# Block sums of k^T v in a windowed linear attention: each block's product made once, three of them added on GpSimd, two tokens taken off by one product

## The chip, the cores and the metric

The kernel runs on one core of a Trainium2 chip. The metric is the time of one execution on the device in microseconds (us), the median of several runs. Beside it stands one profiled execution, whose span and instruction records the profile and the trace show.

## The reference, cut to what matters

The network has four layers on a tensor of 4 batches x 128 channels x 64 x 64. Layers 0 and 1 (a Mamba convolution and a hypergraph convolution) come first; then the data are tokens, 4 batches of 4096 tokens with 128 features, and layers 2 and 3 are an attention and an expert layer each, with a LayerNorm ahead of both and the result added to the tokens. The change concerns the attention of layer 3, a windowed attention without a softmax:

```python
bs, w = (BLOCK_SIZE, WINDOW_SIZE)          # 256, 256
nb = S // bs                               # 16 blocks in a batch
halo = w - 1                               # 255
W = bs + 2 * halo
q = x @ Wq.T + bq
k = x @ Wk.T + bk
v = x @ Wv.T + bv
k_pad = jnp.pad(k, ((0, 0), (halo, halo), (0, 0)))
v_pad = jnp.pad(v, ((0, 0), (halo, halo), (0, 0)))
starts = jnp.arange(nb) * bs
idx = starts[:, None] + jnp.arange(W)[None, :]
k_win, v_win = k_pad[:, idx, :], v_pad[:, idx, :]
q_blk = q.reshape(B, nb, bs, -1)
scale = 1.0 / jnp.sqrt(jnp.float32(D))
attn = jnp.einsum('bnqh,bnkh->bnqk', q_blk, k_win) * scale
out = jnp.einsum('bnqk,bnkh->bnqh', attn, v_win)
...
t = t + _L3_attn_ref(_ln_t(t), L3_attn_Wq, ...)
t = t + _L3_ffn_ref(_ln_t(t), L3_ffn_gate_w, ...)
```

A block of 256 tokens attends to itself and to 255 tokens on either side. So block n sees blocks n-1, n and n+1 but for two tokens: the first token of block n-1 and the last token of block n+1. At the two ends of the sequence the missing block is zero. As there is no softmax, the order of the products is free: out = q (k_win^T v_win) x scale, with one 128x128 matrix M_n = scale x (sum of k^T v over the window's tokens) for each block.

## The kernel before, in words

`tile_kernel` (L1092) runs setup, layers 0 and 1, the first attention (`attn2`), the first expert layer (`ffn` with "L2_ffn"), the second attention (`attn3`, L827 to L909) and the second expert layer (`ffn` with "L3_ffn", which also writes the output). The tokens stay in SBUF throughout as X, 128 partitions x 4 batches x 32 blocks of 128 tokens x 128 features, f32.

The kernel is written in a tile framework. A pool hands out tiles; a tag has a number of buffers, and a tile of the same tag waits for the last reader of the buffer it gets. When a pool closes, its memory is used again by the pools that open later, and the first writer there waits for the last user before. The framework's scheduler decides the order in which instructions stand on each engine, so it isn't the order of the code: an instruction of a later batch or of the next layer can stand ahead of earlier code where its data permit. Each engine then works its queue strictly in order; an instruction that waits holds everything behind it on its engine.

`attn3` loads the three projection weights, transposes them on TensorE (`ps_w`) and loops over 4 batches. A batch has two phases.

- **Chunks.** Eight chunks of 512 tokens (L859). For every 16 blocks of 128 tokens, `ln_stats` (L695) makes the LayerNorm's statistics on VectorE (16 `bn_stats`, L700, then small operations, and a square root on ScalarE, L711). In each chunk VectorE makes four normed blocks `z` (L716, from L866), TensorE transposes them into `ps_z` (L867), ScalarE copies them to `zT` (L868), TensorE makes `ps_q` (L870, evicted by ScalarE into `qT`) and `ps_kv` in two halves (L876, four products in all), and VectorE evicts each half into `kv` with the bias added (L880). Two more VectorE operations a half make `ke` (L885): k of a block with its first token, or its last one, masked to zero.
- **Windows.** Four groups of four windows (L886). For each window TensorE adds up to six products of 128x128 in PSUM (`ps_win`, L896): two for each of the three blocks of 256 tokens, with `ke` in place of k where a token is left out. That makes 92 products in a batch and 368 in the stage. ScalarE copies the four matrices with the scale into `M` (L900), TensorE makes eight products q M (`ps_o`, L905), and VectorE adds them into X (L909).

Buffers: `kv` and `ke` have one buffer, `qT` two, `z` four, `zT` and `M` three; each of the four PSUM tags (`tr`, `ps`, `pm`, `po`) has two.

`ffn` (L911) comes twice. Its route stage handles two batches at a time: `ln_stats`, z (L969), transposes `ps_t` (L970), copies `zTf` on ScalarE and VectorE by turns (L972), the gate's product `ps_l` (L973), the eviction `lg` (L976), then over all tokens the eight largest (L980, L982), two exponentials (L986, L987), their difference (L990), transposes `ps_rt` (L997) and the pooled product `ps_p` (L1003). The experts follow, with weights loaded from HBM (L947 to L952), then the combination: in L2_ffn the products `ps_f` (L1071) and their addition into X (L1072), in L3_ffn L1078, L1082 and the output. The first expert layer thus ends with additions into X, for which the second attention waits, and the second attention ends with additions into X (L909), for which the second expert layer's statistics wait.

Of the kernel before, what the change touches and what calls it, by code (L numbers as in the profile page):

```python
# [7 lines left out]
F32 = mybir.dt.float32  # L8
F16 = mybir.dt.float16
FP8 = mybir.dt.float8e4  # L10
AF = mybir.ActivationFunctionType
ALU = mybir.AluOpType
# [4 lines left out]
P = 128  # L17
# [5 lines left out]
NB = N // P  # L23
# [5 lines left out]
def bc(ap, n):  # L29

    return ap.unsqueeze(1).to_broadcast([ap.shape[0], n, ap.shape[1]])
# [7 lines left out]
class Net:  # L39
# [787 lines left out]
    def attn3(self):  # L827


        nc, tc, a, X = self.nc, self.tc, self.a, self.X  # L830
        BS = 256
        NW = N // BS
        scale = float(C) ** -0.5
        with ExitStack() as ctx:
            wp = ctx.enter_context(tc.tile_pool(name="a3w", bufs=1))
            xp = ctx.enter_context(tc.tile_pool(name="a3x", bufs=1))
            sp = ctx.enter_context(tc.tile_pool(name="a3s", bufs=4))
            tp = ctx.enter_context(tc.tile_pool(name="a3t", bufs=3))
            ps = ctx.enter_context(tc.tile_pool(name="a3ps", bufs=2, space=PSUM))

            wT = wp.tile([P, 3, P], F32, tag="wT", name="wT3")
            pt = ps.tile([P, 3, P], F32, tag="tr", name="ps_w3")
            for k, n in enumerate("qkv"):
                w = tp.tile([P, P], F32, tag="w", name="w3")
                nc.sync.dma_start(w, a[f"L3_attn_W{n}"])
                nc.tensor.transpose(pt[:, k, :], w, self.ident)
            nc.vector.tensor_copy(wT, pt)
            bq = wp.tile([P, 1], F32, tag="bq", name="bq")
            nc.sync.dma_start(bq, a["L3_attn_bq"])
            bkv = wp.tile([P, 2, P], F32, tag="bkv", name="bkv3")  # L850
            for k, n in enumerate("kv"):
                nc.sync.dma_start(bkv[:, k, :], a[f"L3_attn_b{n}"].to_broadcast([P, P]))

            for b in range(B):
                qT = xp.tile([P, N], F32, tag="qT", name="qT3", bufs=2)
                kv = xp.tile([P, NB, 2, P], F32, tag="kv", name="kv3")

                ke = xp.tile([P, NB, P], F32, tag="ke", name="ke")
                for c in range(NCH):  # L859
                    if c % 4 == 0:  # L860
                        nm, rs = self.ln_stats(sp, b, 4 * c, 16)
                    zT = tp.tile([P, 4, P], F32, tag="zT", name="zT3")
                    pt = ps.tile([P, 4, P], F32, tag="tr", name="ps_z3")
                    for i in range(4):
                        z = sp.tile([P, P], F32, tag="z", name="z3")
                        self.normed(z, b, 4 * c + i, nm, rs, (4 * c + i) % 16)  # L866
                        nc.tensor.transpose(pt[:, i, :], z, self.ident)  # L867
                    nc.scalar.copy(zT, pt)  # L868
                    pp = ps.tile([P, CH], F32, tag="ps", name="ps_q")
                    nc.tensor.matmul(pp, wT[:, 0, :], zT.rearrange("p i c -> p (i c)"), start=True, stop=True)  # L870
                    nc.scalar.activation(qT[:, c * CH : (c + 1) * CH], pp, AF.Identity, bias=bq)
                    for h in range(2):
                        j = 4 * c + 2 * h
                        pp = ps.tile([P, 2, 2 * P], F32, tag="ps", name="ps_kv3")
                        for i in range(2):
                            nc.tensor.matmul(  # L876
                                pp[:, i, :], zT[:, 2 * h + i, :], wT[:, 1:3, :].rearrange("p k c -> p (k c)"),
                                start=True, stop=True,
                            )
                        nc.vector.tensor_tensor(  # L880
                            kv[:, j : j + 2, :, :].rearrange("p i k c -> p i (k c)"), pp,
                            bc(bkv.rearrange("p k c -> p (k c)"), 2), ALU.add,
                        )
                        for i, m in enumerate((self.notfirst, self.notlast)):
                            nc.vector.tensor_scalar(ke[:, j + i, :], kv[:, j + i, 0, :], m, None, ALU.mult)  # L885
                for g in range(NW // 4):  # L886
                    pm = ps.tile([P, 4, P], F32, tag="pm", name="ps_win")
                    for i in range(4):
                        n = 4 * g + i
                        terms = [(kv[:, 2 * n, 0, :], 2 * n), (kv[:, 2 * n + 1, 0, :], 2 * n + 1)]  # L890
                        if n > 0:
                            terms += [(ke[:, 2 * n - 2, :], 2 * n - 2), (kv[:, 2 * n - 1, 0, :], 2 * n - 1)]
                        if n < NW - 1:
                            terms += [(kv[:, 2 * n + 2, 0, :], 2 * n + 2), (ke[:, 2 * n + 3, :], 2 * n + 3)]
                        for t, (kk, j) in enumerate(terms):
                            nc.tensor.matmul(  # L896
                                pm[:, i, :], kk, kv[:, j, 1, :], start=t == 0, stop=t == len(terms) - 1
                            )
                    M = tp.tile([P, 4, P], F32, tag="M", name="M")
                    nc.scalar.activation(M, pm, AF.Copy, scale=scale)  # L900
                    for h in range(2):
                        po = ps.tile([P, 4, P], F32, tag="po", name="ps_o3")
                        j = 8 * g + 4 * h
                        for i in range(4):
                            nc.tensor.matmul(  # L905
                                po[:, i, :], qT[:, (j + i) * P : (j + i + 1) * P], M[:, 2 * h + i // 2, :],
                                start=True, stop=True,
                            )
                        nc.vector.tensor_tensor(X[:, b, j : j + 4, :], X[:, b, j : j + 4, :], po, ALU.add)  # L909
# [241 lines left out]
```

## Time and profile before

| | |
|---|---|
| runs | 4511.88, 4515.98, 4558.93 us; median 4515.98 us |
| the profiled execution's own time | 4506.08 us |
| its span in the trace | 4504.3 us |
| TensorE (PE) busy | 3713.7 us, 82% of the span |
| VectorE (DVE) busy | 3124.2 us, 69% |
| GpSimd (POOL) busy | 2415.8 us, 54% |
| ScalarE (ACT) busy | 1981.6 us, 44% |
| second attention | 3963.76 to 4197.06 us |

How to read it: the page gives the busy time of each engine, summed over the whole span, so 82% is a mean over stages that have different limits. The trace gives the same by stretches of time, and the chain of waits follows the work that ended last back from the end, at each step to what released it. In a group of instructions the columns are the line and engine, the operation with output and inputs, the number of records, the busy time in us with the mean of one in ns, and the idle time of the engine just before. A TensorE product of f32 operands leaves two records.

### The profile page before, as it was taken

Reading aid. Unit: us, or ns where it says so; the run is one execution under the profiler, and the core shown is the slowest. Engines: PE = TensorE matmul, PEld = TensorE weight load, DVE = VectorE, ACT = ScalarE, POOL = GpSimd, SP = SyncE. Lnnn points to the kernel's source line nnn. Section 1 sums busy time; section 2 is a strip of 40 time slices with the busy share of each in tenths; the row PEclk is TensorE's granted clock in tenths of the full one; section 3 lists DMA queues with packets and bytes.
Section 4 is the critical chain, followed back from the end, with each engine's and each line's share of the span. In section 5 each row is a group of like instructions: output and inputs, shape, how many; then the busy total and the mean of one; then the engine's idle time right before and its main releaser. Section 6 shows DMA issues by size and latency. Waiting matters only on the chain. (4 is left out here: it accounts for less than half of the span.)

```text
span 4504.3 us, 50176 instructions
## 1 busy us (share of the span) xinstructions
PE 3713.7 (82%) x17975; PEld 2095.2 (47%) x17975; DVE 3124.2 (69%) x5140; ACT 1981.6 (44%) x3104; POOL 2415.8 (54%) x1182
## 2 busy tenths in 40 slices
PE   6887768888887888887878888899977995899778
PEld 2333233345433434543434454456535763578435
DVE  5888889997668999666999866453118985287621
ACT  4655554456445445644544564213225643022221
POOL 5999889887777888677888877300021000000000
PEclk8988878999998899998889999999988997789878
DMA  3455544454464445455455535312250000800044
GB/s 102 155 150 150 143 114 139 124 148 132 126 189 114 125 130 154 122 151 164 113 132 138 153 107 169 119 61 77 76 200 31 1 2 6 297 2 1 2 172 166
DMA packets 261741, 524.36 MB, mean 116 GB/s; under 512 B 21706, under 2 KB 24306, under 8 KB 261490
## 3 DMA queue, kind: packets, MB, share of 16 engines
q1 hardware_dynamic: 250194, 501.78, 37.9%
q10 hardware_dynamic: 11296, 19.37, 1.3%
q8 instruction: 142, 2.33, 0.2%
q14 instruction: 109, 0.89, 0.1%
HBM read 443.47 MB, written 77.59 MB: 116 GB/s over the span
## 5 line engine op out<-in xcount | busy, mean ns | idle before, releaser
L284 POOL TENSOR_TENSOR db<-dx,bt 128x1024 f32<-128x1024 f32 x512 | 1203.0, 2353 | 331.7 <-DVE hs L302 214.6
L302 DVE TENSOR_TENSOR_SCAN hs<-hs,carry,db 128x512 f32<-128x512 f32 x812 | 1035.2, 1282 | 177.5 <-ACT hs L296 95.2
L296 ACT ACTIVATE hs<-dl,A 128x512 f32<-128x512 f32 x1024 | 706.6, 692 | 740.6 <-DVE ho L312 687.1
L497 PE MATMUL ps_g<-xn 128*128 128x512 f32 x1152 | 602.5, 654 | 99.8 <-DVE inc L500 74.3
L319 POOL TENSOR_TENSOR ho_s<-ho_s,ho 128x1024 f32<-128x1024 f32 x288 | 677.1, 2351 | 13.8 <-DVE ho L312 13.1
L312 DVE TENSOR_TENSOR ho<-hs,bt 128x1024 f32<-128x1024 f32 x464 | 563.2, 1214 | 1.6
L520 PE MATMUL ps_ed<-xs,inc 128*128 128x258 f16 x4096 | 513.6, 286 | 18.3 <-ACT inc L513 8.6
L520 PEld LDWEIGHTS <-inc 128*128 128x128 fp8e4 x4096 | 417.8, 102 | 134.6 <-issue 60.6
L500 DVE SCALAR_TENSOR_TENSOR inc<-ps_g,hcl,hb 128x512 fp8e4<-128x512 f32 x576 | 420.3, 736 | 36.7 <-PE ps_g L497 20.9
L497 PEld LDWEIGHTS ps_g<-xn 128*128 128x128 f32 x1152 | 216.0, 204 | 416.6 <-DVE inc L500 182.9
L340 PE MATMUL ps_y<-ho,cst 128*128 128x512 f32 x512 | 274.0, 678 | 108.9 <-POOL ho L308 91.5
L620 PE MATMUL ps_v<-inc_v,es 128*128 128x512 fp8e4 x1536 | 343.1, 383 | 19.2 <-DMA bt<-bcd 17.3
L620 PEld LDWEIGHTS <-es 128*128 128x128 f16 x2048 | 202.7, 99 | 288.9 <-issue 64.1
L513 ACT CAST inc<-ps_t 128x512 fp8e4<-128x512 f32 x448 | 232.1, 600 | 94.5 <-PE ps_t L509 94.3
L222 PE MATMUL ps_c<-xt,wc 128*128 128x512 f32 x512 | 234.9, 613 | 12.6 <-DVE inc L500 6.8
L340 PEld LDWEIGHTS ps_y<-ho,cst 128*128 128x128 f32 x512 | 105.1, 214 | 269.0 <-POOL ho L308 122.6
L526 ACT COPY ed<-ps_ed 128x129 f32<-128x129 f32 x128 | 34.0, 266 | 383.7 <-PE ps_ed L520 383.7
L527 DVE TENSOR_TENSOR ed<-ps_ed,ed 128x129 f32<-128x129 f32 x128 | 36.6, 286 | 211.8 <-ACT ed L526 208.8
L302 DVE TENSOR_TENSOR_SCAN hs<-hs,db 128x512 f32<-128x512 f32 x116 | 141.2, 1223 | 53.6 <-POOL db L284 42.6
L536 POOL TENSOR_TENSOR ed<-ed,rdeg 128x512 f32<-128x512 f32 x32 | 33.3, 1039 | 250.7 <-DVE rdeg L532 250.7
L222 PEld LDWEIGHTS ps_c<-xt,wc 128*128 128x128 f32 x512 | 99.8, 198 | 140.2 <-issue 119.2
L509 PE MATMUL ps_t<-ident,strip 128*128 128x128 fp8e4 x1344 | 115.1, 227 | 51.4 <-ACT inc L513 16.9
(262 smaller groups left out, 5785.5 us busy)
## 6 DMA issues: line engine op xcount, KB each, us to landing
bt<-bcd SPq DMA_DIRECT2D x512, 512.0 KB
inc<-inc SPq DMA_DIRECT2D x192, 256.0 KB
inc_v<-inc SPq DMA_DIRECT2D x96, 512.0 KB
w<-in_L_ffn_weight SPq DMA_DIRECT2D x32, 1024.0 KB
w2f<-in_L_ffn_weight SPq DMA_DIRECT2D x32, 1024.0 KB
strip<-inc SPq DMA_DIRECT2D x84, 256.0 KB
x<-x ACTq DMA_DIRECT2D x32, 256.0 KB
xn<-x SPq DMA_DIRECT2D x32, 256.0 KB
```

Of the source, the lines that this page charges most:

```text
L222: nc.tensor.matmul(s["ps"][h], wc[:, h, j, :], xt[:, j : j + T], start=j == 0, stop=j == 3)
L284: nc.gpsimd.tensor_tensor(db, s["dx"], bc(s["bt", n][:, 0, :], 2), ALU.mult)
L296: act(nc.scalar.activation(hs[:, k, :], s["dl"][:, k, :], AF.Exp, scale=A[:, k, n : n + 1]))
L302: nc.vector.tensor_tensor_scan(to[:, h, :], hs[:, h, :], db[:, h, :], init, ALU.mult, ALU.add)
L312: nc.vector.tensor_tensor(ho, hs, ct, ALU.mult)
L319: nc.gpsimd.tensor_tensor(s["sum", n // G], s["sum", n // G], ho, ALU.add)
L340: nc.tensor.matmul(s["y"][h], self.ident, t[:, h, :], start=False, stop=n == DS - 1 and k == len(terms) - 1,)
L497: nc.tensor.matmul(pq, xn[v // 4][:, v % 4 * P : (v % 4 + 1) * P], xn[c], start=True, stop=True)
L500: nc.vector.scalar_tensor_tensor(inc[:, v, :], pq, hc[:, v : v + 1], hb, ALU.subtract, ALU.is_gt, saturate=False)
L513: later(1, lambda: act(nc.scalar.copy(inc[:, v, :], pt, saturate=False)))
L520: nc.tensor.matmul(pe[:, : 2 * P + 2], inc[:, v, i * P : (i + 1) * P], xs[:, v, :], start=v == 0, stop=v == NB - 1,)
L620: nc.tensor.matmul(pv, es[:, e, k, :], inc[:, e, :], start=e == 0 and k == 0, stop=e == NB - 1 and k == 1,)
```

## The change

The attention's result is the same; the window's matrix is made in another way.

- Each block of 256 tokens gets its product k^T v once: two products of 128x128 (`ps_bl`, L900 of the changed kernel), two blocks in each chunk, right after the chunk's `kv`. ScalarE evicts them with the scale into `bl` (L901), which has a zero block at either end.
- After a batch's chunks, four GpSimd operations (L904 to L907) fill `two`: for each window, k and v of the first token of block n-1 in partitions 0 to 31 and of the last token of block n+1 in partitions 96 to 127. The k part is multiplied with a mask that is -scale on that token and zero elsewhere. Each operation covers 32 partitions x 15 windows x 128 elements. The rest of `two` is set to zero once, by GpSimd (L862).
- For each window one product of `two` (`ps_win`, L911) gives minus the two left-out tokens' part. GpSimd adds the three blocks of `bl` in two additions of 128x512 for a group of four windows (L913, L914), and VectorE adds `ps_win` to it (L915), which gives `M`. `ps_o` and the addition into X stay (L920, L924).
- `ke` and its operations are gone. `two` and `bl` have one buffer each.

Lines of `ffn` stand 15 lower in the changed kernel (L980 is L995).

```diff
@@ -851,11 +853,20 @@
             for k, n in enumerate("kv"):
                 nc.sync.dma_start(bkv[:, k, :], a[f"L3_attn_b{n}"].to_broadcast([P, P]))
 
+
+            masks = wp.tile([P, 2], F32, tag="masks", name="masks")
+            for i, m in enumerate((self.notfirst, self.notlast)):
+                nc.vector.tensor_scalar(masks[:, i : i + 1], m, 1.0, scale, ALU.subtract, ALU.mult)
+
+            two = xp.tile([P, NW, 2, P], F32, tag="two", name="two")
+            nc.gpsimd.memset(two, 0.0)
+
+            bl = xp.tile([P, NW + 2, P], F32, tag="bl", name="bl")
+            nc.gpsimd.memset(bl[:, 0, :], 0.0)
+            nc.gpsimd.memset(bl[:, NW + 1, :], 0.0)
             for b in range(B):
                 qT = xp.tile([P, N], F32, tag="qT", name="qT3", bufs=2)
                 kv = xp.tile([P, NB, 2, P], F32, tag="kv", name="kv3")
-
-                ke = xp.tile([P, NB, P], F32, tag="ke", name="ke")
                 for c in range(NCH):
                     if c % 4 == 0:
                         nm, rs = self.ln_stats(sp, b, 4 * c, 16)
@@ -881,23 +892,27 @@
                             kv[:, j : j + 2, :, :].rearrange("p i k c -> p i (k c)"), pp,
                             bc(bkv.rearrange("p k c -> p (k c)"), 2), ALU.add,
                         )
-                        for i, m in enumerate((self.notfirst, self.notlast)):
-                            nc.vector.tensor_scalar(ke[:, j + i, :], kv[:, j + i, 0, :], m, None, ALU.mult)
+
+                    pm = ps.tile([P, 4, P], F32, tag="pm", name="ps_bl")
+                    for i in range(2):
+                        for h in range(2):
+                            k, v = (kv[:, 4 * c + 2 * i + h, m, :] for m in range(2))
+                            nc.tensor.matmul(pm[:, i, :], k, v, start=h == 0, stop=h == 1)
+                    nc.scalar.activation(bl[:, 2 * c + 1 : 2 * c + 3, :], pm[:, :2, :], AF.Copy, scale=scale)
+                kw = kv.rearrange("p (w i) k c -> p w i k c", i=2)
+                lo, hi = slice(0, 32), slice(96, P)
+                nc.gpsimd.tensor_scalar(two[lo, 1:, 0, :], kw[lo, : NW - 1, 0, 0, :], masks[lo, 0:1], None, ALU.mult)
+                nc.gpsimd.tensor_copy(two[lo, 1:, 1, :], kw[lo, : NW - 1, 0, 1, :])
+                nc.gpsimd.tensor_scalar(two[hi, : NW - 1, 0, :], kw[hi, 1:, 1, 0, :], masks[hi, 1:2], None, ALU.mult)
+                nc.gpsimd.tensor_copy(two[hi, : NW - 1, 1, :], kw[hi, 1:, 1, 1, :])
                 for g in range(NW // 4):
                     pm = ps.tile([P, 4, P], F32, tag="pm", name="ps_win")
                     for i in range(4):
-                        n = 4 * g + i
-                        terms = [(kv[:, 2 * n, 0, :], 2 * n), (kv[:, 2 * n + 1, 0, :], 2 * n + 1)]
-                        if n > 0:
-                            terms += [(ke[:, 2 * n - 2, :], 2 * n - 2), (kv[:, 2 * n - 1, 0, :], 2 * n - 1)]
-                        if n < NW - 1:
-                            terms += [(kv[:, 2 * n + 2, 0, :], 2 * n + 2), (ke[:, 2 * n + 3, :], 2 * n + 3)]
-                        for t, (kk, j) in enumerate(terms):
-                            nc.tensor.matmul(
-                                pm[:, i, :], kk, kv[:, j, 1, :], start=t == 0, stop=t == len(terms) - 1
-                            )
+                        nc.tensor.matmul(pm[:, i, :], two[:, 4 * g + i, 0, :], two[:, 4 * g + i, 1, :], start=True, stop=True)
                     M = tp.tile([P, 4, P], F32, tag="M", name="M")
-                    nc.scalar.activation(M, pm, AF.Copy, scale=scale)
+                    nc.gpsimd.tensor_tensor(M, bl[:, 4 * g : 4 * g + 4, :], bl[:, 4 * g + 1 : 4 * g + 5, :], ALU.add)
+                    nc.gpsimd.tensor_tensor(M, M, bl[:, 4 * g + 2 : 4 * g + 6, :], ALU.add)
+                    nc.vector.tensor_tensor(M, pm, M, ALU.add)
                     for h in range(2):
                         po = ps.tile([P, 4, P], F32, tag="po", name="ps_o3")
                         j = 8 * g + 4 * h
```

## The prediction

> **What bounds the kernel now.** I read the page first: span 4504.3 us, TensorE busy 82%, VectorE 69%, GpSimd 54%. These are averages over stages with different limits, so I next took busy time by stretch over the second attention alone. By the chain of waits it runs from 3963.76 us (last product of the first expert layer, `ps_f`) to 4197.06 us (last addition into X): 233.3 us. The rows cut it at the first `ps_z` of each batch, with the start-up in front and the first expert stage behind.
>
> ```profile
> core 0: us, PE busy (x) PEld busy (x) DVE busy (x) ACT busy (x) POOL busy (x), PEclk, DMA share, GB/s
> 3963.76:3972.04 8.28, 0.93 (x5) 0.51 (x4) 7.81 (x40) 1.59 (x2) 0.00 (x0) 0.50 0.09 16
> 3972.04:4027.58 55.54, 55.23 (x349) 45.63 (x349) 53.77 (x236) 13.52 (x25) 0.00 (x0) 0.96 0.00 1
> 4027.58:4083.08 55.50, 55.16 (x361) 46.09 (x361) 43.58 (x169) 13.78 (x26) 0.00 (x0) 1.00 0.01 1
> 4083.08:4138.57 55.49, 55.26 (x360) 46.14 (x360) 36.61 (x122) 12.65 (x22) 0.00 (x0) 1.00 0.00 1
> 4138.57:4197.06 58.49, 56.88 (x372) 47.62 (x372) 39.67 (x132) 12.61 (x21) 0.00 (x0) 1.00 0.00 1
> 4197.06:4227.92 30.86, 24.75 (x97) 10.19 (x97) 24.11 (x91) 10.35 (x18) 0.00 (x0) 1.00 0.02 4
> ```
>
> TensorE is busy from edge to edge in every batch (55.2 of 55.5 us) and GpSimd does nothing. The chain confirms it; this is one chunk and the window phase of the second batch:
>
> ```profile
> 4053.67 0.67 PE ps_win L896 x6
> 4054.34 1.08 PE ps_q L870 x2
> 4055.42 1.91 PE ps_kv L876 x8
> 4057.32 0.33 PE ps_z L867 x3
> ...
> 4063.20 6.25 PE ps_win L896 x56
> 4069.46 1.85 PE ps_o L905 x16
> 4071.30 5.36 PE ps_win L896 x48
> 4076.66 1.84 PE ps_o L905 x16
> ```
>
> A product of 128x128 f32 is two records, and dense records follow each other every 5.36/48 = 0.112 us, so one product costs 0.223 us. Note that some `ps_win` (x6 to x8) stand inside the chunks: the windows start while the projections still run. The groups of the stage (all of 233.3 us) give the counts:
>
> ```profile
> L896 PE MATMUL ps_win<-kv 128*128 128x128 f32 x496 | 79.7, 275 | 0.0
> L700 DVE BATCH_NORM_STATS2 lnst<-X 128x6 f32<-128x128 f32 x249 | 53.1, 277 | 0.3
> L896 PE MATMUL ps_win<-kv,ke 128*128 128x128 f32 x240 | 46.4, 275 | 0.0
> ```
>
> Here 496+240 = 736 records are 368 products. The 249 statistics are 128 for this stage and 121 that belong to the expert layer behind it: VectorE takes them early, in its idle time.
>
> **What the Trainium skill says.** "GPSIMD Engine Reference", Elementwise and Engine selection: two-input operations cost some 2.6 cycles an element at 1.2 GHz, one-input ones run at about line rate. The trace agrees on the first (128x1024 takes 2353 ns, 2.8 cycles; 128x512 took 1039 ns on L536) and shows no large one-input operation. "SBUF — State Buffer", Who interferes with whom: GpSimd and VectorE lock each other out of a shared port pair if VectorE runs a 2-port mode or reads two SBUF tensors. VectorE here reads PSUM and SBUF, or one SBUF tensor; z of 128 elements takes 340 ns. "VectorE: DVE Perf Modes", the errata section, has (N+151)/0.96: 290 ns at 128, and by the same form 224 ns with half the cycles, so z does not look like a 2-port operation. "TensorE: Matmul & The Clock Gate", Part 1: idle of about 3.4 us halves the clock. Agreed: 8.28 us of idle in the first row stand at clock 0.50, and the first `ps_q` after it took 1.73 us in the chain against 0.86 later.
>
> **The change, part by part.** I used the order in which each engine's instructions stand in the two built programs; nothing differs ahead of the end of the first expert layer (about 3936 us).
>
> (1) TensorE. Out: 368 products x 0.223 = 82.1 us. In: 128 block products and 64 two-token products, 192 x 0.223 = 42.9. Saved 39.2 us, all on the path. A batch then needs 8 chunks x (1.04 q + 1.91 kv + 0.44 z) = 27.1, plus 32 block products 7.1, 16 window products 3.6, 32 `ps_o` 7.4 = 45.2 us, where it was 55.5.
>
> (2) Start-up. In the new order the first batch's statistics and z stand between the X additions of the layer before, where VectorE idles 0.33 or 1.15 us before each; two statistics (0.2 us each) fit. Now `ps_q` starts at 3974.10, 10.3 us after the stage's start. After: wait for the last X addition 0.8, `ps_w` 0.9, four z 0.45, zT copy and latencies 0.75 = 2.9 us. Gain 7.4 us.
>
> (3) The new wait. Four GpSimd operations of 32 partitions x 1920 elements fill `two` once the batch's last kv is evicted, and every `ps_win` of the batch stands behind them on TensorE. Not in the trace. Bounds for one: line rate 1920/1.2 GHz = 1.6 us below (estimate from the skill), the two-input price of L536, 1039/512 x 1920 = 3.9 us, above. I take 2.0, as the work has one input, plus some start cost: 8.0 for four. Counting from the last chunk's kv product: first eviction at 1.9, so GpSimd ends at 1.9+8.0+0.2 = 10.1. TensorE has kv 1.91, bl 0.9, z 0.44, then q 0.95 and kv 1.91 of the next batch, to 6.1, and 12 more z (1.3). Idle: 2.7 us. Behind it on TensorE are q, all `ps_o` and the next batch's bl. VectorE too waits for GpSimd, at the next batch's first kv eviction (`kv` has one buffer), then does two evictions and M: 0.8 us more of waits. So 3.5 us at each of three boundaries, 10.5.
>
> (4) Last batch. Nothing fills: idle to 10.1 is 6.5; then M, `ps_o` and X additions alternate, VectorE's M addition (0.7) now standing between `ps_win` and `ps_o` and behind the earlier X additions: 2.8 more. 9.3 us.
>
> (5) Hidden. The sums for M, 32 GpSimd additions of 1.04 us, are ready early for three groups of four; the fourth stands behind the `two` operations and ends at 10.1+2.1, or once its M buffer is free, before VectorE wants it. The 128 `ke` operations go (30.1 us of VectorE) and are worth nothing, as VectorE isn't the bound; if it were, they'd pay for the 16 M additions (11 us) anyway. ScalarE's 32 evictions of 128x256 replace 16 of 128x512; it is busy 13 of 55 us. The memset of `two` has the first batch's time.
>
> Stage after: 2.5 (start-up without z) + 4x45.2 + 10.5 + 9.3 = 203 us, so 30 us less.
>
> (6) Given back behind it. The new tiles take more SBUF. In the built program the expert layer's first statistic waits for the last M addition, since its tile lies in that memory: the 121 early statistics all move behind the attention. Up to the first maximum (L980) VectorE then has 78 statistics x 0.195 = 15.2, 64 z x 0.27 = 17.3, 8 zTf 5.5, four chains of small operations 2.5: 40.5 us, where the last row shows 30.9. With about 1.5 us of waits for the square roots: 11 us lost. The remaining 50 lie beside the 9 us of exponentials and the 14 us of `ps_rt`/`ps_p`. The expert weights' first loads also move behind the attention; they are needed 137 us later. Seven DMA issues on ScalarE (0.5 to 0.65 us each) come before its first square root, and end as the statistics do.
>
> Sum: 30 - 11 = 19 us. The profiled 4506.08 us (span 4504.3 and 1.8 around it) becomes 4487; it lies 10 us under the median of the three runs, 4515.98, so the time to expect is 4497.
>
> **Rivals.** (B) GpSimd is slow, and the change costs time. Each us more for one `two` operation costs 4x4 = 16 us, so it decides from 2.0+19/16 = 3.2 us on. At the two-input price of 3.9: +30, 11 us slower than before, 4527. For it: the 2.3 ns an element that GpSimd shows, and no one-input row that says otherwise. Against: only one input to read.
> (C) No stall to speak of: `two` at line rate, z covers the wait, and the late statistics sit in TensorE's gaps (24.8 of 30.9 us busy). Then idle falls 6 us, the loss at the back from 11 to 5: 4485. For it: VectorE has been idle 6.8 us of that row. Against: those gaps are waits for VectorE's own results.
> (D) Ports and clock: z are held while GpSimd runs, after all, and the last batch's and the expert stage's idle halve the clock. 14 z late by 2.6 us at three boundaries is 8, clock 3 x 2 us is 6: 4511.
>
> **How the numbers follow.** The forecast 0.50 (4488 to 4508 by itself), B 0.22, C 0.13, D 0.15. The range goes to the two-input price and a little beyond (4532), and at the lower end to C with 9 us for the scatter of runs (4476). One per cent, 45 us, is about what a measurement of this kernel can tell from no change: faster by more asks for all of (1) and (2) with nothing given back, 0.05; slower by more asks for 6 us for each `two` operation, 0.06; within it 0.89.
>
> **What would show it.** Right: `ps_q` some 3 us after the last `ps_f`; 384 records of `ps_bl` and `ps_win`; TensorE idle 2 to 4 us before `ps_win` with GpSimd named as releaser, 6 to 7 in the last batch; 128 statistics in the stage and the rest behind it; the expert layer's first maximum some 41 us after the last X addition. Wrong: `two` operations far from 2.0 us; z longer than 340 ns beside GpSimd; a wait of ScalarE for GpSimd at the `bl` evictions that holds q or zT.

## The result, and the profile after

Over 22 runs of each kernel the median went from 4517.97 to 4581.34 us, and the ratio of the undisturbed runs is 1.0084 (95% interval 1.0054 to 1.0113): some 38 us slower, between 24 and 51. Forecast were 19 us less, so the change ended on the other side. The medians also hold executions in which TensorE's clock in the last stage was about halved (0.53 in the changed kernel's first profile, 0.97 in that of before) and this stage took 136 to 142 us instead of some 80, as it did in the profiles of stats_early, z_act and the three kernels below whose names begin with actc_stats; the ratio leaves most such executions out, and the profile below is a second one of the changed kernel, taken without that (4522.92 us, span 4521.1).

Busy time by stretch, cut where TensorE starts again after its wait at the end of a batch: the start-up to the first `ps_q`; the first batch's chunks; then twice the windows of one batch with the chunks of the next; the third batch's windows with the whole of the fourth; and the route stage to the first maximum. Columns are the stretch, its length, then busy time and records of PE, PEld, DVE, ACT and POOL, TensorE's granted clock, DMA share and GB/s.

```profile
core 0: us, PE busy (x) PEld busy (x) DVE busy (x) ACT busy (x) POOL busy (x), PEclk, DMA share, GB/s
3966.16:3969.66 3.50, 2.23 (x9) 1.84 (x10) 3.13 (x10) 0.58 (x1) 3.43 (x3) 0.50 0.22 40
3969.66:4021.71 52.05, 40.92 (x192) 29.04 (x191) 47.92 (x149) 15.14 (x30) 21.44 (x10) 0.89 0.00 0
4021.71:4079.34 57.63, 49.77 (x281) 39.11 (x282) 47.92 (x108) 14.46 (x28) 24.02 (x12) 0.91 0.00 1
4079.34:4136.92 57.58, 49.83 (x274) 38.65 (x273) 38.72 (x61) 13.02 (x25) 23.98 (x12) 0.89 0.00 1
4136.92:4207.78 70.86, 56.54 (x341) 46.63 (x339) 30.53 (x54) 10.15 (x20) 26.41 (x14) 0.87 0.00 1
4207.78:4259.89 52.11, 33.63 (x97) 12.79 (x97) 39.99 (x183) 11.33 (x20) 0.00 (x0) 0.74 0.25 83
```

TensorE issues far less (274 to 281 records from one boundary to the next, 360 before), yet that takes 57.6 us where it took 55.5, because TensorE is idle for 7.8 us of it and runs at 0.9 of its clock. From the last addition of the layer before to the last addition into X it is 241.6 us (before 232.6 by the same cut), and from there to the first maximum 52.1 (30.9). The first profile of the changed kernel has 241.7 and 52.1. These two stretches give 9 + 21 = 30 us, within the interval of the ratio; the later stages differ from before by no more than the two profiles of the changed kernel differ there.

The chain of waits at the second boundary:

```profile
4061.78 1.92 PE ps_kv L887 x8
...
4067.07 10.46 DVE z L716 x6
...
4077.66 1.68 PE ps_z L878 x6
```

and at the end of the last batch:

```profile
4178.85 1.00 POOL two L904
...
4183.92 1.77 POOL two L905
...
4185.77 5.12 POOL two L906
...
4190.93 1.79 POOL two L907
...
4192.77 2.93 PE ps_win L911 x12
```

In the last batch TensorE has almost nothing left to do: of the 13.9 us from GpSimd's first operation to the windows it is idle for 12.5. At the inner boundaries the chain names z of VectorE instead. What GpSimd does in that time is in its timeline:

```profile
4063.47 5.11 POOL L904 TENSOR_SCALAR two<-kv,masks 32x1920 f32<-32x1920 f32 x1 [0.83 <-DVE kv L891]
4068.55 1.81 POOL L905 COPY two<-kv 32x1920 f32<-32x1920 f32 x1
4070.43 5.17 POOL L906 TENSOR_SCALAR two<-kv,masks 32x1920 f32<-32x1920 f32 x1
4075.65 1.78 POOL L907 COPY two<-kv 32x1920 f32<-32x1920 f32 x1
```

and VectorE's:

```profile
4064.33 14.97 DVE L716 TENSOR_SCALAR z<-X,lnnm,lnrs 128x128 f32<-128x128 f32 x14
```

The two multiplications take 5.1 us each, more than the upper bound of 3.9, and the two copies 1.8; the four take 13.85 us, where the prediction had 8.0. Beside them fourteen z, which need about 0.27 us each when dense, take 15 us. By source line the stage's z read

```profile
L716 DVE TENSOR_SCALAR z<-X,lnnm,lnrs x124: 324/340/5069, 3967.6 to 4171.1; 128x128 f32<-128x128 f32 x124
```

(shortest, median and longest in ns; before, the longest was 347). The longest z is as long as a GpSimd multiplication. The groups of the stage, against those of the prediction:

```profile
L900 PE MATMUL ps_bl<-kv 128*128 128x128 f32 x256 | 41.5, 286 | 0.6 <-DVE kv L891 0.5
L700 DVE BATCH_NORM_STATS2 lnst<-X 128x6 f32<-128x128 f32 x95 | 22.2, 285 | 0.0
L911 PE MATMUL ps_win<-two 128*128 128x128 f32 x128 | 21.4, 335 | 12.2 <-POOL two L907 12.2
```

256 + 128 = 384 records replace 736, as worked out. A `ps_win` takes 335 ns in the mean instead of 275, because the first group of windows behind a wait runs slowly. At the second boundary the clock was 1.00 in the 4.3 us ahead of the wait; then 16 records of `ps_win` took 3.41 us in the chain, at clock 0.50, and the next 16, some 8 us later, 1.79 us at 1.00:

```profile
4079.34:4082.75 3.41, 3.41 (x18) 3.41 (x17) 1.85 (x3) 0.14 (x1) 0.00 (x0) 0.50 0.02 5
4087.73:4089.52 1.79, 1.79 (x18) 1.71 (x17) 1.38 (x2) 0.00 (x0) 0.93 (x1) 1.00 0.00 0
```

The statistics in the stage are 95 instead of 249.

### The profile page after: what moved, and what is told of

It is laid out like the page before. It is cut to its first block, busy times and chain, and to the rows that moved or that the text cites. A ratio compares the mean times of both kernels' runs of the same rounds, so it can differ in the third digit from the quotient of the medians.

```text
span 4602.8 us, 49529 instructions
## 1 busy us (share of the span) xinstructions
PE 3759.7 (82%) x17623; PEld 2098.7 (46%) x17623; DVE 3142.6 (68%) x5030; ACT 1984.6 (43%) x3120; POOL 2516.6 (55%) x1233
## 5 line engine op out<-in xcount | busy, mean ns | idle before, releaser
L222 PE MATMUL ps_c<-xt,wc 128*128 128x512 f32 x512 | 237.4, 618 | 13.9 <-DVE inc L500 6.8
L862 POOL MEMSET two<- 128x4096 f32 x1 | 3.5, 3512 | 333.9 <-ACT lnrs L711 333.9
```

What stands on the lines that cost most here:

```text
L222: nc.tensor.matmul(s["ps"][h], wc[:, h, j, :], xt[:, j : j + T], start=j == 0, stop=j == 3)
```

## The experiments

Theory: three things, in order of size. The wait for `two` is long because a GpSimd multiplication costs 5.1 us; the expert layer's late statistics cost 21 us; and GpSimd's work holds z, which adds a little. Rivals: the hold of z is the main cost, or TensorE's clock and the sums on GpSimd are.

Each run is read by the two stretches in its own profile: in the two profiles of the changed kernel they repeat to 0.1 us, while the start of the attention lies anywhere from 3947 to 3988 us in the profiles here. Times in us; ratio is of the undisturbed runs to those of before, with its 95% interval, where there were enough.

| kernel | four operations on two | attention | to the first maximum | both | ratio |
|---|---|---|---|---|---|
| before | none | 232.6 | 30.9 | 263.4 | 1 |
| the change | 13.85, GpSimd | 241.6 | 52.1 | 293.7 | 1.0084 (1.0054 to 1.0113) |
| stats_early | 13.85, GpSimd | 240.8 | 37.2 | 278.0 | 1.0105 (1.0055 to 1.0155) |
| z_act | 13.85, GpSimd | 235.0 | 50.8 | 285.8 | one run |
| two_tt | 10.3, GpSimd | 230.7 | 51.8 | 282.5 | one run |
| two_copy | 7.1, GpSimd | 216.6 | 50.8 | 267.4 | one run |
| two_act4 | 7.3, ScalarE | 227.1 | 51.8 | 278.8 | 1.0065 (1.0040 to 1.0090) |
| actc | in chunks, ScalarE | 198.3 | 51.0 | 249.3 | 0.9976 (0.9943 to 1.0009) |
| actc_stats | in chunks, ScalarE | 197.2 | 34.2 | 231.4 | 0.9830 (0.9736 to 0.9924) |
| actc_stats_sumdve | in chunks, ScalarE | 195.3 | 35.0 | 230.2 | none |
| actc_stats_sumdve_zact | in chunks, ScalarE | 209.1 | 34.3 | 243.3 | 0.9932 (0.9869 to 0.9995) |
| kinds (of before) | see below | 237.1 | 50.8 | 287.8 | 1.0069 (1.0023 to 1.0114) |

**after_again**: the changed kernel, no edit.

> The changed kernel once more, for a second profile. If the stretch of the attention and of the route stage behind it are what makes it slower, both read as in the first profile (about 242 us from the last addition of the layer before to the last addition into X, and about 52 us from there to the first maximum), and nothing else differs by more than 5 us from the kernel before. If the cost lies in TensorE's clock in the last stage (62 pairs of ps_f at 4.0 us in the first profile, 2.1 us before), the attention and route stretches still differ but the sum of all stages doesn't match.

The first reading held for the two stretches: 241.6 and 52.1 us. The last stage takes 80.1 us (before 80.5), so nothing is lost there. That nothing else would differ by more than 5 us did not hold: the expert stage, from its first `ps_eo` to the first `ps_f`, takes 74.7 us here, 89.8 before and 93.6 in the first profile of the changed kernel. That is why this profile's span is only 17 us above that of before; since two profiles of one kernel differ there by 19 us, it isn't put down to the change.

**kinds**: GpSimd's price by kind of operation, and what it holds, on the kernel before.

```diff
+dead = xp.tile([P, 15, P], F32, tag="dead", name="dead")
...
+lo = slice(0, 32)
+nc.gpsimd.tensor_copy(dead[lo, 0, 0:1], kv[lo, NB - 1, 1, 0:1])
+for r in range(4):
+    src = X[lo, 3, 0:15, :]
+    if b == 0:
+        nc.gpsimd.tensor_scalar(dead[lo], src, self.notfirst[lo], None, ALU.mult)
+    elif b == 1:
+        nc.gpsimd.tensor_copy(dead[lo], src)
+    elif b == 2:
+        nc.gpsimd.tensor_tensor(dead[lo], src, src, ALU.add)
+    else:
+        nc.gpsimd.tensor_scalar(dead[lo], kv[lo, 0:15, 0, :], 2.0, None, ALU.mult)
```

> The kernel before, with four GpSimd operations of 32 partitions x 1920 elements after each batch's last kv, into a dead tile that nobody reads: batch 1 multiplies with a per-partition operand, batch 2 copies, batch 3 adds two inputs, batch 4 multiplies with a constant. Theory 1 (an operation has its price by kind, and VectorE's z waits for the whole of a GpSimd operation): 5.1, 1.8 and about 4 us, the constant like the operand; single z of about the length of the GpSimd operation beside them; yet the attention stays within 3 us of 233, since TensorE has window products to work on meanwhile, so being held is not what costs. Theory 2 (being held costs): the attention grows by 5 to 10 us. Theory 1 for the statistics: the dead tile takes memory, so the expert layer's statistics stand behind the attention here too, and the time grows by 15 to 21 us though the attention's own products are those of before.

The records of the dead tile (durations in ns, shortest, median, longest):

```profile
L892 POOL TENSOR_SCALAR dead<-X,cst x4: 5107/5108/5112, 4022.0 to 4037.6; 32x1920 f32<-32x1920 f32 x4
L894 POOL COPY dead<-X x4: 1773/1775/1776, 4085.6 to 4091.1; 32x1920 f32<-32x1920 f32 x4
L896 POOL TENSOR_TENSOR dead<-X x4: 3375/3376/3377, 4141.1 to 4151.5; 32x1920 f32<-32x1920 f32 x4
L898 POOL TENSOR_SCALAR dead<-kv x4: 5033/5034/5035, 4196.6 to 4211.9; 32x1920 f32<-32x1920 f32 x4
```

An operation with a scalar costs 2.7 ns an element whether the scalar is an operand or a constant, a copy 0.9, and the addition of a tile to itself 1.8. So the price doesn't go by the number of inputs: the dearest kind and the cheapest have one each. No z fell beside them here, but other work of VectorE's did:

```profile
4022.26 4.99 DVE L886 TENSOR_SCALAR ke<-kv,cst 128x128 f32<-128x128 f32 x2
...
4037.91 3.33 DVE L707 TENSOR_TENSOR lnrs<-lnst 128x16 f32<-128x16 f32 x1
```

Two `ke` took 0.46 us elsewhere in this trace and a `lnrs` 0.17. So operations with scalars from SBUF to SBUF, and one with two SBUF inputs, lasted until GpSimd's instruction ended, whatever their own size. Not all did: another `lnrs` and two `lnd` beside GpSimd kept their 0.17 to 0.18 us. The additions into X, which read PSUM, keep their 0.69 us in the same stretch. The attention grew by 4.5 us, between the two expectations, so this run doesn't say what a hold costs. It does show the other loss alone: with the attention's own products unchanged, the dead tile moved the statistics behind it and the stretch to the first maximum went from 30.9 to 50.8 us.

**two_tt** and **two_copy**: the wait for two shortened in two steps.

```diff
-nc.gpsimd.tensor_scalar(two[lo, 1:, 0, :], kw[lo, : NW - 1, 0, 0, :], masks[lo, 0:1], None, ALU.mult)
+nc.gpsimd.tensor_tensor(two[lo, 1:, 0, :], kw[lo, : NW - 1, 0, 0, :], mk[lo, 0, :, :], ALU.mult)
```

for two_tt, where `mk` is the mask broadcast over windows and row, and for two_copy, which leaves the mask out,

```diff
-nc.gpsimd.tensor_scalar(two[lo, 1:, 0, :], kw[lo, : NW - 1, 0, 0, :], masks[lo, 0:1], None, ALU.mult)
+nc.gpsimd.tensor_copy(two[lo, 1:, 0, :], kw[lo, : NW - 1, 0, 0, :])
```

with the same in `two[hi]`.

> The changed kernel with the mask multiplied by a two-input operation of GpSimd (the mask broadcast over the row) instead of the operation with a per-partition operand; the result is the same. If the price goes by the kind of operation, as in the run of the four kinds (3.4 us for two inputs, 5.1 with an operand), the four take 10.3 us a batch and the attention falls by 4 x 3.5 = 14 us, to 225 to 231 us. If the broadcast input costs as much as the operand did, nothing changes.

> The changed kernel with the two multiplications by a mask replaced by plain copies on GpSimd; this leaves the mask out, so 32 tokens are taken off at each end of a window instead of one. The four operations then take 4 x 1.8 = 7.2 us a batch instead of 13.8, near the 8.0 us that the prediction took. Theory 1 (the price of the multiplication is what the prediction missed): 6.6 us less in each of four batches, so the attention falls by 20 to 28 us, to 214 to 222 us. Rival (the hold of z, TensorE's clock and the sums would have kept it long at the predicted price too): it stays above 228 us.

The multiplications took 3.38 us as two-input operations, and 1.78 us as copies. The attention of two_copy, with the columns as above:

```profile
3957.94:4174.56 216.62, 197.93 (x1091) 155.46 (x1091) 149.61 (x378) 53.42 (x102) 72.22 (x51) 0.93 0.01 1
```

From 13.85 to 10.3 to 7.1 us a batch the attention goes from 241.6 to 230.7 to 216.6: 25.0 us for 6.7 us less in four batches, 3.7 us for each us (3.1 in the first step, 4.4 in the second). Theory 1 holds for the size: the price, with the wait and the hold that come of it, is worth 25 us of the attention.

**two_act4**: the same four operations on ScalarE.

```diff
-nc.gpsimd.tensor_scalar(two[lo, 1:, 0, :], ..., masks[lo, 0:1], None, ALU.mult)
-nc.gpsimd.tensor_copy(two[lo, 1:, 1, :], ...)
+nc.scalar.activation(two[lo, 1:, 0, :], ..., AF.Identity, scale=masks[lo, 0:1])
+nc.scalar.copy(two[lo, 1:, 1, :], ...)
```

> The four operations on two go to ScalarE, same shapes; GpSimd keeps the sums. Theory 1 (the wait is GpSimd's own speed, 13.8 us a batch): an operation takes 1.5 to 2.0 us, the wait for two falls to 6 to 8 us a batch, z is no longer held by them, and the time falls by 20 to 30 us. Rival 1 (the cost is elsewhere: late statistics and TensorE's clock after any idle): the attention falls by less than 10 us. Rival 2 (ScalarE's queue: zT, qT and bl stand behind the four operations): the time falls by 5 to 15 us only, and TensorE waits for zT.

They take 1.9 and 1.77 us there, 7.3 together, and the attention falls by 14.5: less than theory 1 said, and 10.5 us longer than two_copy with the same total on GpSimd. Rival 2 is right about the order, but not about the wait. At the second boundary ScalarE's next copy of `zT` starts only when the fourth operation ends (4077.9 us), so TensorE has no products of the next batch to fill the time with; the wait that it shows is for `two`, not for zT: 5.5 to 5.7 us in each batch, 22.3 in all, where in two_copy the waits at the ends of the four batches, for z or `two`, add up to 13.8. That is 8.5 of the 10.5 us.

**z_act**: z on ScalarE, so that GpSimd can't hold it.

```diff
-self.normed(z, b, 4 * c + i, nm, rs, (4 * c + i) % 16)
+nc.scalar.activation(z, X[:, b, 4 * c + i, :], AF.Identity, bias=nr[:, q : q + 1], scale=rs[:, q : q + 1])
```

> The changed kernel with z made on ScalarE (one operation with scale and bias a block, as many as before), so that VectorE's z can't be held by GpSimd; the GpSimd operations stay at 5.1 and 1.8 us. In the changed kernel TensorE's window products wait for two until it is done, and for the held z 1.9 us more. Theory 1 (the speed of the four operations is the cost, the hold adds little): the attention falls by 3 to 10 us from 241.6, no more. Rival (the hold is the main cost): it falls by over 15 us, towards the 227.1 us of the run with the four operations on ScalarE.

```profile
3970.67:4205.68 235.01, 193.54 (x1091) 155.49 (x1091) 101.24 (x255) 96.66 (x226) 98.86 (x51) 0.90 0.01 1
```

6.6 us less, within theory 1's 3 to 10. What TensorE waits for shows why; these are the longest sums of waits in the attention, of the changed kernel and of z_act (us in total, times, longest):

```profile
PE ps_z L878 <- DVE z L716: 26.6, 12, 8.0
PE ps_win L916 <- POOL two L912: 34.0, 4, 12.2
```

Of the 26.6 us, 25.4 lie at the three inner boundaries. With no z to hold, TensorE waits there for `two` itself, 34.0 less the 12.2 of the last batch = 21.8 us. So although the chain named z, `two` would have been late almost as long: the hold is real and secondary. The 6.6 us are a net figure, since z on ScalarE has a cost of its own (the last run below).

**stats_early**: the expert layer's statistics in a pool of their own, opened ahead of the attention.

```diff
+net.s3 = ctx.enter_context(tc.tile_pool(name="s3", bufs=4))
 net.attn3()
...
-st[r] = self.ln_stats(sp, 2 * p + r, 4 * c, 16)
+st[r] = self.ln_stats(sp if out is None else self.s3, 2 * p + r, 4 * c, 16)
```

> The changed kernel with the expert layer's LayerNorm statistics in memory of their own, so that they needn't wait for the last M addition. Theory 1 (late statistics cost what the profile shows, 52 us instead of 31 to the first maximum): some 100 statistics move into the attention, the stretch falls to 33 to 36 us and the time by 15 to 20 us. Rival (VectorE is blocked by GpSimd inside the attention, so early statistics only lengthen it): the stretch falls as well, but the attention grows by as much, and the time moves by less than 5 us.

The stretch fell from 52.1 to 37.2 us, a little above the 33 to 36 expected, and the attention didn't grow (240.8), so the early statistics are free and late ones cost 15 of the 21 us. What is left shows in the chain:

```profile
4228.17 4.88 DMA gw<-in_L_ffn_gate_w
```

The gate's weights are loaded only at the end of the attention, in both kernels; now the first expert weights, moved to the same moment, share the DMA engines with them (34% busy in this stretch, 2% before). That the sharing makes the load slow is likely, but no run keeps the two apart. The ratio doesn't show the gain: at 1.0105 (1.0055 to 1.0155) its interval overlaps that of the change. Stretches outside the change move by more than this gain (the start of the attention above), so the claim rests on the profile alone.

**actc** and **actc_stats**: k and v of the left-out tokens made on ScalarE in each chunk, right after its `kv`; the sums stay on GpSimd.

```diff
-nc.vector.tensor_scalar(masks[:, i : i + 1], m, 1.0, scale, ALU.subtract, ALU.mult)
+nc.vector.tensor_scalar(masks[:, i : i + 1], m, 1.0, -(scale ** 0.5), ALU.subtract, ALU.mult)
...
+n = min(2 * c + 3, NW)
+nc.scalar.activation(two[lo, 2 * c + 1 : n, :, :], kw[lo, 2 * c : n - 1, 0, :, :], AF.Identity, scale=masks[lo, 0:1])
+n = max(2 * c - 1, 0)
+nc.scalar.activation(two[hi, n : 2 * c + 1, :, :], kw[hi, n + 1 : 2 * c + 2, 1, :, :], AF.Identity, scale=masks[hi, 1:2])
...
-nc.vector.tensor_tensor(M, pm, M, ALU.add)
+nc.vector.tensor_tensor(M, M, pm, ALU.subtract)
```

> As actc_stats without the separate memory for the statistics, so they stand behind the attention again. Theory 1 (the two losses are independent): the attention takes 192 to 200 us, as in actc_stats or a little less, the stretch to the first maximum 50 to 53 us instead of 34, and together they are 245 to 252 us: with the wait for two gone the change is faster than before (263.5 us) even with the late statistics. Rival (the statistics inside the attention are what lengthens it): the attention falls to under 187 us.

> The two left-out tokens' k and v are made on ScalarE chunk by chunk (two operations of 32 partitions x 512 each chunk, k and v scaled alike with the square root of the scale, and the product subtracted), so that the last part is ready about 1 us after the last kv; statistics in memory of their own; the sums stay on GpSimd. Theory 1 (waiting for two is what made the attention long): TensorE's idle time in the attention falls from 42 to under 20 us, its clock rises from 0.88 to over 0.95, the attention takes 200 to 212 us, the stretch to the first maximum 33 to 38 us, and both together are 20 to 30 us less than before the change (263.5 us). Rival (the sums on GpSimd, 1.27 us each, hold z and come late themselves): the attention stays over 220 us, and TensorE waits for M.

The two stretches of actc_stats:

```profile
3976.22:4173.46 197.24, 184.93 (x1091) 148.66 (x1091) 160.31 (x501) 95.57 (x170) 44.20 (x35) 0.98 0.01 2
4173.46:4207.62 34.16, 26.47 (x97) 10.92 (x97) 23.66 (x85) 10.17 (x17) 0.00 (x0) 0.90 0.38 127
```

TensorE's idle time is 197.24 - 184.93 = 12.3 us where it was 42.3, and its clock 0.98. The attention is somewhat below the low end of theory 1; both stretches are 32 us shorter than before the change, where 20 to 30 were expected. The measured ratio is 0.983 (0.9736 to 0.9924), faster than before by 0.8 to 2.6%; 32 us are 0.7%, just outside it. The ratio rests on two executions of this kernel, and what else was shorter in them isn't known, so the stretches are the safer size. Without the separate memory (actc) the attention is the same and the stretch behind it 51.0, so the two losses are independent; that kernel's ratio, 0.9976, can't be told from before.

**actc_stats_sumdve** and **actc_stats_sumdve_zact**: the sums on VectorE, then z on ScalarE as well.

```diff
-nc.gpsimd.tensor_tensor(M, bl[:, 4 * g : 4 * g + 4, :], bl[:, 4 * g + 1 : 4 * g + 5, :], ALU.add)
-nc.gpsimd.tensor_tensor(M, M, bl[:, 4 * g + 2 : 4 * g + 6, :], ALU.add)
+nc.vector.tensor_tensor(M, bl[:, 4 * g : 4 * g + 4, :], bl[:, 4 * g + 1 : 4 * g + 5, :], ALU.add)
+nc.vector.tensor_tensor(M, M, bl[:, 4 * g + 2 : 4 * g + 6, :], ALU.add)
```

> As actc_stats, with the sums on VectorE instead of GpSimd (32 additions of 128x512, 0.7 us each). If GpSimd's sums cost anything (held z, late M), the attention is 3 to 10 us shorter than in actc_stats. If VectorE becomes the bound (22 us more work on it), it is longer, and fewer statistics stand early.

> As actc_stats_sumdve, with z on ScalarE too. If VectorE is the bound there, this takes 36 us of work off it and the attention gets 3 to 10 us shorter. If ScalarE's queue becomes the bound (z, zT, qT, two and bl in order, some 27 us a batch more), it gets longer.

The sums on VectorE gave 2 us, under the 3 that were expected if GpSimd's sums cost anything: they are all but hidden. With z on ScalarE too the attention is 14 us longer: ScalarE's busy time there rises from 96 to 144 us, and TensorE now waits 8.5 us for its `qT` and 7.2 for its `zT`. What was taken off VectorE didn't show, as VectorE wasn't the bound.

## Why the prediction was wrong

**Where it failed.** Step (3): "I take 2.0, as the work has one input, plus some start cost". The two copies cost that (1.8 us), the two multiplications 5.1: a mean of 3.46 us, past the 3.2 from which rival (B) was said to decide. The bounds were also too low, since the upper one came from a two-input operation and was taken for the dearest kind. By the slope of two_copy, 3.7 us of attention for each us a batch, (13.85 - 8.0) x 3.7 = 22 us of the 39 by which the stage lies over the 203 forecast (242.3 us from the last `ps_f`, as the prediction cut it).

**The other 17 us of the attention.** The 203 us were 181 us of products, four times the "45.2 us" of step (1), and some 22 us of waits. The changed kernel has 199.3 us busy and 42.3 idle. In two_copy, with 7.1 us for the four operations instead of 8.0, the idle time is 216.6 - 197.9 = 18.7 us; 0.9 us more in each of four batches gives some 22 (an estimate from these rows). At the right price the waits of (2) to (4) would thus have come out. TensorE's busy time would not: it stays at 197.9 us. So the second failed step is the 45.2 us a batch in (1), the price of dense products for a TensorE that now stops at the end of each batch. In actc_stats, where it doesn't wait for `two`, as many records are busy 184.9 us, at clock 0.98. The halved clock behind each wait is a part of the difference that is shown (1.6 us for the first 16 `ps_win` of the second boundary, and the `ps_z` ahead of them stand at 0.50 too); how the rest divides between the clock and short gaps inside the chunks, the runs don't separate.

The prediction knew of a halved clock, but carried it only in rival (D), with 6 us. What it took as agreement in its first row isn't: of the "8.28 us of idle" 0.93 are busy, and the clock had been at 0.50 before, with TensorE busy all the time:

```profile
3940.00:3963.76 23.76, 23.76 (x133) 23.05 (x132) 11.66 (x17) 0.00 (x0) 0.00 (x0) 0.50 0.00 1
```

It had also dismissed the hold, because a z of 340 ns "does not look like a 2-port operation". A duration taken with nothing beside it can't show that, and the section that it cites gives (N+151)/0.96 for an f32 addition of two tensors, not for z's operation. What the Trainium skill says in "SBUF — State Buffer", Who interferes with whom, fits what the trace now shows: the one blocks the other for the whole of an instruction, and `tensor_scalar` is named there among the operations that can take the shared pair (z up to 5069 ns against 347). By z_act it cost little beside the wait for `two`.

**Step (6), the statistics.** This is the third failed step. The mechanism was right, and is shown alone by stats_early and by kinds; the size was off, 21.2 us for 11. VectorE's work was 40.0 us against 40.5 forecast. The wrong term is "about 1.5 us of waits": it is 12.1 us (52.1 - 40.0). The largest in VectorE's timeline are these:

```profile
4212.89 0.23 DVE L70 COPY gwT<-ps_tr 128x64 f32<-128x64 f32 x1 [3.34 <-PE ps_tr L69]
...
4250.89 0.69 DVE L987 COPY zTf<-ps_t 128x512 f32<-128x512 f32 x1 [2.92 <-PE ps_t L985]
```

The first is the late load of the gate's weights, the others copies that stand in VectorE's order ahead of what it could do. The row of before already had 30.86 - 24.11 = 6.7 us of such waits, which should have been carried along.

**What held.** (1): 384 records instead of 736. (2): the first `ps_q` starts 3.5 us after the last addition into X, 4.2 after the last `ps_f`; 2.9 were forecast and 10.3 before, so 6 us gained for 7.4. (4) had the right shape, and its wait for two is 12.5 us idle instead of 6.5. (5): the sums and M are all but hidden, as actc_stats_sumdve shows, though an addition took 1.27 us instead of 1.04. At the second boundary TensorE idles 7.8 us (15.0 us with 7.2 busy), at the others 9.9 and 7.7, where 2.7 were forecast.

**The rivals.** (B) happened, with the hold and the halved clock of (D) on top. (B) gave 4527 us for 3.9 us an operation, 11 over before; at a mean of 3.46 it was 30, since (B) carried over the sum's other shortfalls. The "Elementwise" and "Engine selection" sections of the "GPSIMD Engine Reference", from which the 2.0 came, give 2.6 cycles an element for two inputs and about line rate for one; here a copy agrees with the second (0.93 ns an element), and an operation with a scalar, one input too, costs 2.66 ns, 3.2 cycles at the page's 1.2 GHz.

## What to carry to other kernels

An engine's price goes by the kind of operation; where the trace has no row of that kind, put the dearest known row's price well inside the range, and keep what waits for it short by making it in pieces as its input arrives: here the same work in chunks on ScalarE, with the statistics early again, turned a loss of 30 us over the two stretches into a gain of 32. When a new tile grows a pool, look at what in the next layer was early because that memory was free. If a chain names one engine, ask what else was late at that moment: z ended last, yet with z made elsewhere TensorE waited for `two` instead, 21.8 of the 25.4 us. And price the products behind a new wait at the pace that they have there, not at the dense one: the busy time fell by 24 us (223.4 to 199.3), where 39 were forecast.

## What the runs showed of the hardware that I had not expected

- GpSimd on 32 partitions x 1920 f32: an operation with a scalar 5.03 to 5.17 us, one with the same tile twice or a broadcast second input 3.38, a copy 1.78. An addition of two different tiles of 128x512 took 1.27 us (2.5 ns an element).
- ScalarE did the same multiplication in 1.89 us, and in pieces of 32 x 512 in 0.72.
- While GpSimd ran, most of VectorE's operations with scalars from SBUF to SBUF (z, `ke`) and one with two small SBUF inputs (`lnrs`, 0.17 us alone) lasted until GpSimd's instruction ended, 1.7 to 5.1 us; additions with one input from PSUM kept their 0.69 us.
- With 7.7 to 12.5 us of idle time of TensorE at the end of each batch its clock was 0.87 to 0.91 over a batch; it was 0.98 over the attention when the idle time was cut to 12.3 us in all. Short waits were enough: at the second boundary of two_copy TensorE was busy for 0.33 of 2.31 us, and the next 3.41 us ran at clock 0.53; ahead of the wait it was 1.00.
